# Turning the first sequence's rows in 32 x 32 squares on VectorE and moving them by DMA, in place of 16 TensorE transposes

## The chip, the cores and the metric

The kernel runs on one core of one Trainium2 chip. A core has TensorE (in the profile PE, with its weight loads as PEld), VectorE (DVE), ScalarE (ACT), GpSimd (POOL) and the sync engine (SP), which here only starts DMAs. ACT and POOL can start DMAs too. The metric is the device time of one launch in microseconds (us); less is better.

## The reference, cut to what matters

Two transformer layers run over an input x of 2 sequences x 512 rows x 512 columns, with a layer norm behind each of four parts: memory attention, a ternary feed-forward, softmax attention, a plain feed-forward. Only the end of the first part and the beginning of the second matter here:

```python
q_sel = (elu(x @ Wq.T + bq) + 1)[every 4th head]      # 8 heads of 128
num = einsum('bshd,hde->bshe', q_sel, M)
den = einsum('bshd,hd->bsh', q_sel, z) + 1e-6
x = layernorm(x + repeat(num / den, 4 heads) @ Wo.T)   # "reading"
gate, up = (x / 128) @ w_gate.T, (x / 128) @ w_up.T    # first feed-forward
x = layernorm(x + trunc(clip(down(trunc(silu(gate) * up)))))
```

The feed-forward truncates, so its products must be exact enough: each row x is split into a rounded part `hi` and a remainder `lo = x - hi`, and both are multiplied by the weights, which the kernel has found to be ternary.

## The kernel before, in words

**Tiles.** A sequence b is 4 tiles of 128 rows (`xs[b][t]`, 128 partitions x 512 columns, float32). The 8 tiles stand in the list `order`; tile i below is `order[i]`, so tiles 0 to 3 are the first sequence and 4 to 7 the second.

**The reading stage** is the loop `for i, (b, t) in enumerate(order)` at line 553. `read` (L419) makes, for tile i, 8 matmuls of 128 x 512 (L428), one for each head, into a PSUM bank each; there are 8 banks in all (`psum`, L81). They go in two groups of four heads, called g0 and g1 below. For each group ACT writes the four denominators (`den`, L432), DVE inverts them (L436), and then the banks are read: heads 0 to 2 by ACT into `y` (L441; three buffers), which POOL adds up (L445), and heads 3 to 7 by DVE, each with one instruction that adds into x (L450). Only then is a bank free for a head of the next tile. At the end POOL adds y into x (L457). The layer norm of tile i-1 lies within tile i (`norm_a0`, L526): statistics on DVE (L137, L139), the inverse root on POOL (L145, L146), an offset on DVE (`off`, L534), and the scaling of the row on ACT (L535).

**Turning the rows.** The feed-forward needs x with its columns on the partitions. For the first sequence TensorE did this: `split(0)` is called in tile 5, and its `block(k)`, two in tile 5 and two in tile 6, transposes four 128 x 128 blocks into a PSUM bank (L273), then ACT writes `hi` (L278) and DVE writes `lo` (L279) from that bank. For the second sequence DVE turns each tile in 32 x 32 squares as soon as it is normed (`turn_squares`, L549, instruction L551, into the tile `squares`), and `move_squares` (L284) then puts the squares in their places with 16 DMAs of 64 KB, in pieces of 128 bytes: 9 from SP's queue, 4 from POOL's, 3 from ACT's (L292). `split(1, xt1)` reads the result from SBUF behind the first four chunks of the feed-forward (L721).

**What sets the order.** POOL's instructions, and the DMAs that it starts, run as the program writes them (`manual_schedule`, L61). The instructions of PE, ACT and DVE are put in order by the framework's planner when the kernel is compiled; on the chip each engine then works through its list strictly in turn, and an instruction that must wait holds up all behind it. `tc.issue_after(x)` makes instructions of x's own engine stand behind x in that list.

**Buffers.** The pool `xtp` has two rooms of 128 x 2048 floats (tag `xt`), which are used in turn: the turned inputs `xt_a00` and `xt_a01`, then `xh_0` (the four `hi` blocks of the first sequence), then `squares`. The read queries are 16 tiles of 128 x 512 (tag `q`, L391), one for each sequence and head.

**Behind the reading stage**, `up(0, c)` for chunks c = 0 to 5 and then `up(1, 0)` multiply `hi` and `lo` by the weights (L611): per chunk four products of `hi` and four of `lo`, for the gate and again for the up part.

Of the kernel before, what the change touches and what calls it, by code (L numbers as in the profile page):

```python
# [10 lines left out]
F32 = mybir.dt.float32  # L11
# [8 lines left out]
P = 128  # L20
B, S, HID = 2, 512, 512
NT = S // P
NK = HID // P
NH, G, D = 8, 4, 128
# [6 lines left out]
SQ = 32  # L31
# [7 lines left out]
def kernel(  # L39
# [19 lines left out]
    nc = tc.nc  # L59
# [6 lines left out]
    xtp = ctx.enter_context(tc.tile_pool(name="xtp", bufs=2))  # L66
# [5 lines left out]
    ident = const.tile([P, P], F32, tag="ident", name="ident")  # L72
# [8 lines left out]
    def psum(name):  # L81
        return ps.tile([P, 512], F32, tag="mm", name=name)


    xs = [[], []]
# [171 lines left out]
            wds.append(wd)  # L257
        return wds

    def split(b, xt=None):  # L260


        hi = xtp.tile([P, NK, S], F32, tag="xt", name=f"xh_{b}").bitcast(F32R)
        los = [pair_tile(f"xl_{b}_{i}").bitcast(F32R) for i in range(2)]
        his = [hi[:, k, :] for k in range(NK)]
        los = [los[k // 2][:, k % 2, :] for k in range(NK)]

        def block(k):
            h, l = his[k], los[k]
            if xt is None:  # L270
                rows = psum(f"pt_f0{b}_{k}")
                for t in range(NT):
                    nc.tensor.transpose(rows[:, ts(t, P)], xs[b][t][:, ts(k, P)], ident)  # L273
            else:
                rows = xt[:, :, k, :]
                h, l = (u.rearrange("p (t q) -> p t q", t=NT) for u in (h, l))
            return (
                nc.scalar.copy(h, rows),  # L278
                nc.vector.tensor_sub(l, rows, h.bitcast(F32)),  # L279
            )  # L280

        return his + los, block
# [17 lines left out]
    def pair_tile(name):  # L300
        return wop.tile([P, 2, HID], F32, tag="wo", name=name)
# [6 lines left out]
    with tc.tile_pool(name="a0w", bufs=1) as a0w, tc.tile_pool(name="a0", bufs=2) as a0:  # L308
# [59 lines left out]
        def first_queries(pq, xt):  # L368

            done = first_rows(xt, 0)  # L370
            for t in range(NT):
                if t + 1 < NT:
                    with tc.issue_after(done.ins):
                        done = first_rows(xt, t + 1)
                with tc.issue_after(done.ins):
                    done = query_products(pq, xt, 0, ts(t, P))
            return done

        def queries(b, xt, h):

            pq = psum(f"pq_{b}_{h}")
            if b == h == 0:
                done = first_queries(pq, xt)
            else:
                done = query_products(pq, xt, h, slice(0, S))

            e = a0.tile([D, S], F32, tag="e", name=f"e_{b}_{h}")
            nc.scalar.activation(e, pq, AF.Exp, bias=bq[:, h : h + 1])  # L388
            r = a0.tile([D, S], F32, tag="r", name=f"r_{b}_{h}")
            nc.scalar.activation(r, pq, AF.Relu, bias=bq[:, h : h + 1])  # L390
            q = a0.tile([D, S], F32, tag="q", name=f"q_{b}_{h}", bufs=16)  # L391
            nc.vector.scalar_tensor_tensor(q, e, 1.0, r, ALU.min, ALU.add)
            qs[b].append(q)
            return done
# [84 lines left out]
            )  # L479

        checks = [(c, a) for c in range(len(CHUNKS)) for a in range(2)]
        qs = [[], []]
        xt = xtp.tile([P, NK, S], F32, tag="xt", name="xt_a00")
        with tc.issue_after(queries(0, xt, 0).ins):
            queries(0, xt, 1)
        for h in range(2, NH):
# [5 lines left out]
            elif h == 6:  # L492
                xt1 = transposed(xs[1], "a01")
# [31 lines left out]
        order = [(b, t) for b in range(B) for t in range(NT)]  # L525
# [23 lines left out]
        def turn_squares(i):  # L549
            b, t = order[i]  # L550
            nc.vector.transpose(squares[:, t, :], xs[b][t])  # L551

        for i, (b, t) in enumerate(order):
            steps = read(b, t, lambda steps: norm_a0(i - 1, steps) if i else None)
            for _ in range((3, 2, 2, 0, 0, 0, 0, 0)[i]):
                check_up(*checks.pop(0))
            if i == 3:
                tot_up = total(counts, "up")
            elif i == 4:
                flag_up, eff_up = verdict(tot_up, sc_up, "up")  # L560
            if i >= len(order) - LEAD:
                for a in range(2):
                    divided(i - len(order) + LEAD, a)
            if i == 5:
                parts, block = split(0)
                x2.append(parts)
                squares = xtp.tile([P, NT, HID], F32, tag="xt", name="squares")
            if i in (5, 6):
                for k in range(2):
                    block(2 * (i - 5) + k)  # L570
            if i > NT:
                turn_squares(i - 1)
        norm_a0(len(order) - 1, steps)
        turn_squares(len(order) - 1)
# [14 lines left out]
    xt1 = fp.tile([P, NT, NK, P], F32, tag="it11", name="xt_f01", bufs=1)  # L589
# [4 lines left out]
    with tc.tile_pool(name="f0", bufs=2) as f0:  # L594
# [123 lines left out]

        for c in range(LEAD - 2):
            up(0, c, [cut_off[f"f00_{c - 2}"]] if c > 1 else ())  # L720
        parts, block = split(1, xt1)  # L721
# [157 lines left out]
    for b in range(B):  # L879
# [5 lines left out]
        xt = xt_a1[b]  # L885
# [4 lines left out]
        for j in range(2):  # L890
            p = psum(f"pqk_{b}_{j}")
# [11 lines left out]
        for t in range(NT):  # L903
            p = psum(f"pv_{b}_{t}")
# [167 lines left out]
    t = NT - 1  # L1072
# [161 lines left out]
    steps = [(0, 0), (0, 1), (0, 2), (1, 0), (1, 1), (1, 2)]  # L1234
# [86 lines left out]
```

## Time and profile before

| What | us |
|---|---|
| median of 3 runs (lowest, highest) | 470.58 (470.02, 470.64) |
| the profiled execution's own time | 470.72 |
| its span in the trace | 468.7 |
| PE busy in the span | 461.0 (98%) |
| reading matmuls L428, 128 records | 57.1 |
| PE transposes of the first sequence L273, 16 records | 114.7 to 123.8 from the span's start |
| first product of the feed-forward | from 131.2 |
| DMAs of the second sequence's squares, started | 141.2 to 148.2 |
| first product of the second sequence | from 153.0 |

The profiled execution took 2.0 us more than its span, which is what lies around it. The granted clock of TensorE was 0.998. In the lists of the trace each line has a start in us from the span's start, a length in us, the engine, the line of the kernel and what it writes from what it reads; in square brackets stands how long the engine had been idle before and who ended that. A float32 matmul of the reading is recorded as two, so 8 heads are 16 records.

### The profile page before, as it was taken

How to read it: one execution, taken by the hardware profiler on the slowest of the kernel's cores; microseconds unless marked ns; L12 is line 12 of the kernel's file. 1: busy time of each engine (PE TensorE's matmuls, PEld its weight loads, DVE VectorE, ACT ScalarE, POOL GpSimd, SP SyncE). 2: the span in 40 equal slices, each digit the busy share in tenths (PEclk: the TensorE clock that was granted, in tenths of full speed). 3: DMA queues.
4: the chain of work that ended last, by engine and by line, in shares of the span. 5: the costliest groups of instructions: out<-in, count | busy, mean ns of one | idle time of the engine just before them, and what ended most of it. 6: DMA issues, size and time to landing. Idle time of an engine off the chain costs nothing.

```text
span 468.7 us, 5727 instructions
## 1 busy us (share of the span) xinstructions
PE 461.0 (98%) x1883; PEld 329.0 (70%) x1883; DVE 329.5 (70%) x627; ACT 267.5 (57%) x507; POOL 115.1 (25%) x144
## 2 busy tenths in 40 slices
PE   9999999999999999999999999999999999999994
PEld 8454444434478888888866567888888888888884
DVE  1165677767876767775979889895755778998632
ACT  3344799557756767456756842584645768443101
POOL 0235101566543053600357032000000000050111
PEclk9999999999999999999999999999999999999999
DMA  8989900000006500051390000000000000001001
GB/s 284 381 297 363 387 9 0 0 0 3 1 1 134 201 1 3 11 162 45 91 390 31 0 1 1 1 0 1 1 0 1 0 1 1 1 24 45 37 31 45
DMA packets 21651, 35.02 MB, mean 75 GB/s; under 512 B 9840, under 2 KB 10736, under 8 KB 21616
## 3 DMA queue, kind: packets, MB, share of 16 engines
q1 hardware_dynamic: 19616, 33.73, 20.7%
q10 hardware_dynamic: 1872, 0.56, 0.5%
q8 instruction: 22, 0.36, 0.3%
q0 software_dynamic: 128, 0.26, 0.3%
q14 instruction: 13, 0.11, 0.1%
HBM read 31.40 MB, written 2.10 MB: 71 GB/s over the span
## 4 chain that ended last, share of the span: by engine, by line
PE 71%; ACT 7%; DVE 5%; issue 3%; POOL 0%; POOLq 0%; DVEq 0%; ACTq 0%
PE pm L1111 17%; PE pg_f L611 9%; PE pu_f L611 9%; PE pc L1111 8%; PE pdm L1199 7%; PE pd_f L666 4%; PE pdc L1199 4%; DVE x L450 3%; PE pqk L893 3%; PE po L428 2%; ACT y L441 2%; ACT t L463 2%; PE pv L906 2%; PE pot L989 1%; PE po L1005 1%
## 5 line engine op out<-in xcount | busy, mean ns | idle before, releaser
L428 PE MATMUL po<-mw,q 128*128 128x512 f32 x128 | 57.1, 598 | 0.3 <-DVE mv_a L139 0.2
L352 PE MATMUL pq<-xt_a,wq 128*128 128x512 f32 (+1 forms) x152 | 56.9, 526 | 0.0
L145 POOL TENSOR_TENSOR rstd_f<-mv_f,ln_eps 128x1 f32<-128x1 f32 x15 | 4.4, 293 | 169.3 <-DVE mv_f L1214 130.2
L428 PEld LDWEIGHTS po<-mw,q 128*128 128x128 f32 x128 | 22.9, 189 | 32.1 <-issue 17.7
L352 PEld LDWEIGHTS pq<-xt_a,wq 128*128 128x128 f32 x152 | 26.2, 190 | 27.4 <-issue 25.7
L1111 PE MATMUL pm<-r,ugu 128*128 128x512 f32 x152 | 37.7, 389 | 0.0
L1111 PE MATMUL pm<-r,it_early 128*128 128x512 f32 x144 | 36.7, 392 | 0.0
L1111 PEld LDWEIGHTS pm<-r,ugu 128*128 128x128 f32 x152 | 28.5, 188 | 5.9
L1111 PEld LDWEIGHTS pm<-r,it_early 128*128 128x128 f32 x144 | 27.0, 188 | 6.1 <-issue 0.5
L169 ACT ACTIVATE ta_f<-y_f,below_half 128x512 int8<-128x512 f32 (+1 forms) x22 | 15.9, 721 | 27.0 <-DVE y_f L157 26.7
L450 DVE SCALAR_TENSOR_TENSOR x<-po,den,x 128x511 f32<-128x511 f32 x40 | 29.8, 745 | 1.9
L1121 DVE SCALAR_TENSOR_TENSOR ev_q<-pm,ev_q 128x512 f32<-128x512 f32 x27 | 18.6, 688 | 14.4 <-PE pm L1111 14.4
L637 DVE SCALAR_TENSOR_TENSOR it_f<-tb_f,ta_f 128x512 fp32r<-128x512 int16 (+1 forms) x22 | 15.4, 702 | 18.3 <-ACT tb_f L170 18.3
L445 POOL TENSOR_TENSOR y<-y,y 128x511 f32<-128x511 f32 x16 | 20.3, 1271 | 31.5 <-ACT y L441 30.8
L388 ACT ACTIVATE e<-pq,bq 128x512 f32<-128x512 f32 x16 | 11.1, 692 | 24.1 <-PE pq L352 20.6
L611 PE MATMUL pg_f<-xh,tu 128*128 128x512 f32 x88 | 24.3, 398 | 0.0
L1120 ACT ACTIVATE ev_q<-pc 128x512 f32<-128x512 f32 x27 | 16.0, 593 | 14.2 <-PE pc L1111 14.1
L465 POOL TENSOR_SCALAR td<-wd,inv_down 128x512 fp32r<-128x512 f32 x11 | 18.2, 1668 | 22.1 <-DVE inv_down L205 22.1
L611 PE MATMUL pg_f<-xl,tu 128*128 128x512 f32 x88 | 23.6, 390 | 0.0
L611 PE MATMUL pu_f<-xh,tu 128*128 128x512 f32 x88 | 23.5, 389 | 0.0
L611 PE MATMUL pu_f<-xl,tu 128*128 128x512 f32 x88 | 23.5, 389 | 0.0
L1001 ACT ACTIVATE x<-x,off_f,rstd_f 128x512 f32<-128x512 f32 x7 | 5.7, 816 | 27.7 <-POOL off_f L1000 27.7
(315 smaller groups left out, 1087.5 us busy)
## 6 DMA issues: line engine op xcount, KB each, us to landing
gu<-in_gu SPq DMA_DIRECT2D x20, 512.0 KB, 7.9
wo<-in_wo SPq DMA_DIRECT2D x16, 512.0 KB, 6.9
wd<-in_wd SPq DMA_DIRECT2D x20, 256.0 KB, 4.5
wq<-in_wq SPq DMA_DIRECT2D x8, 256.0 KB, 4.9
x<-in_x SPq DMA_DIRECT2D x7, 256.0 KB, 5.4
out<-x SPq DMA_DIRECT2D x7, 256.0 KB, 2.0
wqkv<-in_wqkv SPq DMA_DIRECT2D x1, 768.0 KB, 10.8
xt_f<-squares SPq DMA_DIRECT2D x9, 64.0 KB, 2.4
```

The costliest lines, as they stand in the source:

```text
L169: nc.scalar.activation(a[:n], y, AF.Relu, bias=below_half[:n])
L352: done = nc.tensor.matmul(pq[:, at], wq[h][:, k, :], xt[:, k, at], start=(k == 0), stop=(k == NK - 1),)
L428: nc.tensor.matmul(po, qs[b][h0 + j][:, ts(t, P)], mw[:, h0 + j, :], start=True, stop=True,)
L445: nc.gpsimd.tensor_add(ys[0][:, :LAST], ys[0][:, :LAST], y[:, :LAST])
L450: steps.append(nc.vector.scalar_tensor_tensor(x[:, :LAST], four[j][:, :LAST], d, x[:, :LAST], ALU.mult, ALU.add))
L465: eng.tensor_scalar(out, w, factor, None, ALU.mult)
L611: nc.tensor.matmul(pp[a], t[:, a, i % NK, :], x2[b][i], start=(i == 0), stop=(i == 2 * NK - 1),)
L666: nc.tensor.matmul(pd, inter[b][c][:, ts(t, P)], td[c].bitcast(F32R), start=(c == 0), stop=(c == last),)
L1111: nc.tensor.matmul(p, w, x, start=(left[id(p)] == begun[id(p)]), stop=(left[id(p)] == 1))
L1120: nc.scalar.activation(ev, pc, AF.Copy, scale=CROSS)
L1121: nc.vector.scalar_tensor_tensor(ev, pm, MAIN, ev, ALU.mult, ALU.add)
L1199: nc.tensor.matmul(p[:, :w], got[j // 4][1][kind][:, j % 4], down_parts[j][kind][:, cols], start=(j == 0 and kind == kinds[0]), stop=(j == ...
```

## The change

The first sequence's rows are now turned as the second's are. After each of the tiles 1 to 4 (i), `turn_first(i - 1)` has DVE turn the tile that was normed last, in squares, into a new tile `squares0` of the pool `xtp`, laid out so that four row tiles' pieces of one square lie next to each other. At i = 4 `move_first` starts 16 DMAs of 64 KB in pieces of 512 bytes, 6 from POOL's queue and 10 from SP's, into `xt_f00`. This takes the room of the read queries of heads 0 to 3 of the first sequence, which are now one tile of four heads. The PE transposes are gone. The `hi` and `lo` instructions read `xt_f00` from SBUF, all four blocks are written in tile 7, and those of DVE stand behind the first L450 of tile 7. `squares` now takes the room of `squares0`, and `xh_0` that of `xt_a01`.

```diff
-    def split(b, xt=None):
+    def split(b, xt):
...
         def block(k):
-            h, l = his[k], los[k]
-            if xt is None:
-                rows = psum(f"pt_f0{b}_{k}")
-                for t in range(NT):
-                    nc.tensor.transpose(rows[:, ts(t, P)], xs[b][t][:, ts(k, P)], ident)
-            else:
-                rows = xt[:, :, k, :]
-                h, l = (u.rearrange("p (t q) -> p t q", t=NT) for u in (h, l))
+            rows, order = xt(k)
+            h, l = (
+                u.rearrange(f"p (t i c) -> p {order}", t=NT, c=SQ) for u in (his[k], los[k])
+            )
...
-            q = a0.tile([D, S], F32, tag="q", name=f"q_{b}_{h}", bufs=16)
+            if b == 1:
+                q = a0.tile([D, S], F32, tag="q", name=f"q_{b}_{h}", bufs=8)
+            else:
+                if h % 4 == 0:
+                    qs0.append(a0.tile([D, 4, S], F32, tag=f"q0_{h // 4}", name=f"q0_{h}", bufs=1))
+                q = qs0[-1][:, h % 4, :]
...
+        squares0 = xtp.tile([P, NK, P // SQ, NT, SQ], F32, tag="xt", name="squares0")
+
+        def turn_first(t):
+            out = squares0.rearrange("p k j t c -> p (k j) t c")[:, :, t, :]
+            nc.vector.transpose(out, xs[0][t].rearrange("p (b c) -> p b c", c=SQ))
+
+        def move_first():
+
+            xt = a0.tile([P, NK, P // SQ, NT, SQ], F32, tag="q0_0", name="xt_f00", bufs=1)
+            for i in range(P // SQ):
+                for j in range(P // SQ):
+                    eng = nc.gpsimd if (4 * i + j) % 3 == 0 else nc.sync
+                    eng.dma_start(
+                        xt[ts(j, SQ), :, i].rearrange("p k t c -> p k (t c)"),
+                        squares0[ts(i, SQ), :, j].rearrange("p k t c -> p k (t c)"),
+                    )
+            return xt
...
             if i == 5:
-                parts, block = split(0)
+                parts, block = split(0, lambda k: (xt0[:, k], "i t c"))
                 x2.append(parts)
                 squares = xtp.tile([P, NT, HID], F32, tag="xt", name="squares")
-            if i in (5, 6):
-                for k in range(2):
-                    block(2 * (i - 5) + k)
-            if i > NT:
+            if i == len(order) - 1:
+                with tc.issue_after(steps[0].ins):
+                    for k in range(NK):
+                        block(k)
+            if 0 < i <= NT:
+                turn_first(i - 1)
+            if i == NT:
+                xt0 = move_first()
+            elif i > NT:
                 turn_squares(i - 1)
```

More of the change, by code (lines that the diff above doesn't have):

```diff
@@ L481 @@
         checks = [(c, a) for c in range(len(CHUNKS)) for a in range(2)]
-        qs = [[], []]
+        qs, qs0 = [[], []], []
         xt = xtp.tile([P, NK, S], F32, tag="xt", name="xt_a00")
@@ L720 @@
             up(0, c, [cut_off[f"f00_{c - 2}"]] if c > 1 else ())
-        parts, block = split(1, xt1)
+        parts, block = split(
+            1, lambda k: (xt1[:, :, k].rearrange("p t (i c) -> p t i c", c=SQ), "t i c")
+        )
         x2.append(parts)
```

## The prediction

> **What bounds the kernel now.** I read the page first: the busy times, then the shares of the chain that ended last.
>
> ```profile
> PE 461.0 (98%) x1883; PEld 329.0 (70%) x1883; DVE 329.5 (70%) x627; ACT 267.5 (57%) x507; POOL 115.1 (25%) x144
> ...
> PE 71%; ACT 7%; DVE 5%; issue 3%; POOL 0%; POOLq 0%; DVEq 0%; ACTq 0%
> ```
>
> TensorE is the bound almost everywhere. A share of the whole says nothing of this stage, so next the chain of waits around the edit (start, us, what):
>
> ```profile
> 116.50 0.75 DVE x L450
> 117.25 0.06 DVE st_a L137
> 117.31 0.46 issue
> 117.77 0.73 DVE x L450
> ...
> 118.65 4.53 PE po L428 x10
> 123.18 0.88 PE pt_f L273 x8
> 124.05 1.73 PE po L428 x4
> ...
> 126.07 0.62 ACT tu L463
> 126.69 4.53 PE po L428 x10
> 131.22 1.86 PE pg_f L611 x8
> ```
>
> From 118.65 on the chain lies on PE, the removed transposes (L273) are a link of it, and it runs on into the feed-forward (L611) without a hole. So PE time taken out before 131.2 moves the end, if nothing else becomes late. Then the timeline of 112 to 131, for what is near to being late:
>
> ```profile
> 113.19 0.81 ACT L535 ACTIVATE x<-x,off,rstd_a 128x512 f32<-128x512 f32 x1 [0.59 <-DVE off L534]
> 115.23 2.62 POOL L445 TENSOR_TENSOR y<-y,y 128x511 f32<-128x511 f32 x2 [0.84 <-ACT y L441]
> 116.22 0.18 DVE L436 RECIPROCAL den<-den 128x4 f32<-128x4 f32 x1 [2.12 <-ACT den L432]
> 118.67 0.19 POOL L145 TENSOR_TENSOR rstd_a<-mv_a,ln_eps 128x1 f32<-128x1 f32 x1 [0.82 <-DVE mv_a L139]
> 121.00 0.20 DVE L534 TENSOR_SCALAR off<-mv_a,rstd_a 128x1 f32<-128x1 f32 x1
> ```
>
> DVE has a hole of 2.12 us before the second reciprocal of tile 5, and POOL little room between its adds and the root that DVE's `off` needs. Last, the existing turn and move, as the tile `squares` shows them (ns min/median/max, first and last start):
>
> ```profile
> L292 SPq DMA_DIRECT2D xt_f<-squares x9: 627/645/1769, 141.3 to 148.2; - x9
> L551 DVE STREAM_TRANSPOSE squares<-x x4: 694/711/712, 122.1 to 140.4; 128x512 f32<-128x512 f32 x4
> L292 POOL DMA_DIRECT2D xt_f<-squares x4: 648/654/996, 141.9 to 144.2; - x4
> ```
>
> **The change part by part.** The sum is made against the profiled execution, 470.72 (span 468.7 and 2.0 around it); the median shown, 470.58, is 0.14 lower.
>
> *Transposes removed.* In the timeline eight of them occupy PE from 114.72 to 115.59, the next eight from 123.02 to 123.89: 0.87 each, **-1.75** in all, on the chain.
>
> *What they drag behind them.* A reading record costs 0.43 on PE (weight loads at 113.00, 113.43, 113.86), 16 of them 6.88. From 115.59 to 123.02 stand 16 records: 7.43, so 0.55 is lost; from 123.89 to the last one's end slot (about 131.05) 7.16, 0.28 lost. PE waits there for banks, held because casts (L278, 0.55 apart) and subtractions (L279, 0.66) stand between the denominators and the L450s, and because two banks hold transposed rows. In tile 6 casts and subtractions are gone afterwards: **-0.55**. In tile 7 four of each come instead of two: I count the 0.28 as kept.
>
> *DVE: four turns, 0.71 each if the spread-out writing costs nothing.* That pattern is not in the trace; the nearest rows of 512 columns are 0.68 (L137) and 0.75 (L450), so 2.7 to 3.0 for four. After the scaling of its tile (ACT L535) ends at 93.0, 100.3 and 114.0, DVE stands idle until 95.38, 102.55 and 116.22: three of four are covered. Tile 2's scaling ends at 107.83, amid the verdict; there the second reciprocal of tile 4 (109.26) slips by about 0.5, but PE has its banks of tile 5 in hand (no wait shown from 107.8 to 114.7). Cost 0; without that cover 0.7.
>
> *16 DMAs.* They can start when tile 3 is turned: 114.0 + 0.1 + 0.71 = 114.9. SP has nothing else to start before 141. A DMA with 128 pieces is not shown from SBUF to SBUF; a load with 128 rows starts every 0.49 (8 in 3.94 at 148.9), those with 512 pieces every 0.83 (9 in 7.50). I take 0.49, since the number of pieces is equal: ten are started by 119.8. Landing took 2.1 to 4.4, so the rows are there at 121.9 to 124.2, at worst (0.83, 4.4) 127.6. The casts want them at about 124 to 127.
>
> *POOL.* Its six DMAs go in front of tile 5's adds. By its row, 0.65 and 0.08 between: 4.4 us; by the load row of SP, 0.33 and 0.08, 2.5. They run from 114.9 (POOL is idle from 114.4 to 115.23), so the adds end at 120.0 to 121.9 in place of 117.85, and the root of tile 4, with 0.9, is ready at 120.9 to 122.8. `off` and behind it L535 of tile 4 want it at 119.8 (121.00 less two subtractions that leave). Against 1.1 to 3.0 us of lateness stands slack: without transposes PE reaches tile 7's first head at 122.4, when that bank would have been free since 121.55, so 0.85 is free. If the planner puts the reciprocal and the y's of tile 6 ahead of this `off`, as it put L436 and an L450 ahead of `off` at 105.6, the lateness costs nothing. So 0 to 2.1; I take **0**, as the planner sees POOL's list, and keep 2.1 for the range.
>
> [...]
>
> *Room of `squares`.* It is now that of `squares0`, so the turn of tile 4 (122.08 before, about 121 now) must wait until the DMAs have read it. DVE's hole there lasts to about 122.7: 0 if landed by 122, 1.5 at 124.2 if this turn stands first; I take 0.
>
> *The end of the stage.* PE is through with tile 7 at 131.05 - 2.3 = 128.75 and wants the first `lo` 0.91 later (four products of `hi`), the fourth at 130.34. DVE's first L450 of tile 7 (129.42 before) ends at about 127.8; four subtractions, 0.61 apart (2.50 for four from SBUF at 151.58), end at 130.25. If the turn of tile 5 stands ahead of them, 130.96: **+0.6**. I take that; it is 0 without. The casts (4 x 0.55) must then fit into ACT's list ahead.
>
> *Second sequence.* DVE's subtractions and turn (3.16) stand where a turn and 1.47 of idling stood (2.18), so its last turn comes 2.3 - 0.98 = 1.3 earlier, PE 1.7 earlier. Its last `lo` ended at 154.08 and was wanted at 153.02 + 0.91 + 0.68 = 154.61: the 0.53 of slack covers the 0.4. Cost 0.
>
> Sum: -1.75 - 0.55 + 0.6 = -1.7; 470.72 - 1.7 = **469.0**.
>
> [...]
>
> **The rivals.**
>
> *(a) POOL gives it back.* `off` of tile 4 stays ahead of tile 6's reciprocal, and DVE waits for the root behind six DMA issues. For it: program order on POOL, and the gap of only 0.8 before 115.23. Against it: the planner has swapped such pairs. Price up to 2.1: 469.0 + 2.1 = 471.1 at worst, with mid prices 470.5. PE's waits would then name y or L450 in tile 7.
>
> *(b) Slower: ACT's casts reach the head of its list before the rows land.* Only DVE's half is tied behind tile 7's first L450; ACT's is free to stand among the denominators of tile 6, at about 119.3. ACT is then held to the landing, 121.9 to 124.2, and with it the y's that free the banks; less 0.85 of slack, 1.8 to 4.1: about 472 (-1.7 + 3). It decides if the casts stand before tile 6's y's and the landing is after 121.5. Against it: the planner counts DMA time as well.
>
> *(c) The loop of DVE and ACT takes over from PE.* Tile 2 to 3 took 7.17 between second reciprocals (95.38 to 102.55), tiles 6 and 7 8.04. If they fall to 7.17 and no further, the gain is 1.74 in place of 2.3: 469.6 with the 0.6 at the end. Against it: tiles 4 and 5 ran at 6.7 and 7.0.
>
> *(d) It doesn't do what it says.* Hardly possible: the instructions are gone from PE's list.
>
> **How the numbers follow.** The forecast (468.2 to 469.5) 0.45; (c) 0.13; (a) 0.22; (b) 0.15; the rest, 0.05, a gain beyond 2.3. A change of under 0.2%, 0.94 us, can hardly be told from none. Faster: 0.45 + 0.13 and a part of the rest, 0.60; the same: (a), 0.22; slower: (b) and the worst of (a), 0.18. The range reaches from all of 1.75 + 0.83 and no wait (468.1) to (a) at its worst (471.2), and leaves out (b).
>
> **What would show it.** Right: no L273; the feed-forward's first product at about 129.5 in place of 131.2, all of the gain before it and the same distance from there to the end. (a): a long wait of DVE's `off` for the root around 120, POOL's issues right before. (b): ACT's cast with an idle time ended by a DMA. Room: L551 of tile 4 waiting for a DMA. End: PE's weight load of `pg_f` waiting for `xl`. The prediction is wrong above all if the six issues on POOL or the landing lie on the chain.

## The result and the profile after

The changed kernel takes 477.89 us (median of 5 runs, 476.30 to 477.99), the kernel before 470.58 beside it: a ratio of 1.0142, 95% interval 1.0131 to 1.0154. It is 1.4% slower. The forecast was 469.0, in a range up to 471.2, so it has the wrong sign, and the time lies beyond every rival. The profiled execution took 476.74, its span is 475.0. Below, L numbers are those of the changed kernel: L429 is the reading matmul (L428 before), L437 the reciprocal, L442 y, L446 and L458 POOL's adds, L451 DVE's adds, L274 and L275 the `hi` casts and `lo` subtractions, L535 `off`, L567 the new DMAs, L636 the products of the feed-forward. In the experiments they shift by a few lines. A gate product is eight matmuls, four of `hi` and four of `lo`; an up product is the same for the up part.

From the page of the changed kernel, the busy times and the chain's shares:

```profile
PE 462.6 (97%) x1867; PEld 328.2 (69%) x1867; DVE 333.9 (70%) x631; ACT 267.7 (56%) x507; POOL 119.5 (25%) x150
...
PE 74%; DMA 8%; ACT 5%; DVE 5%; issue 3%; POOL 2%; SPq 2%; POOLq 0%; DVEq 0%; ACTq 0%
```

PE has 16 instructions fewer (1867 for 1883) and is busy 1.6 us longer. DVE's busy time grew by 4.4, though four turns at 0.71 make only 2.8. So instructions have become longer on both engines. The chain's shares now name POOL and SP's queue with 2% each, but no place; that is found in the timeline of PE, from the last heads of the reading on:

```profile
125.31 1.13 PE L429 MATMUL po<-mw,q 128*128 128x512 f32 x2 [0.56 <-ACT y L442]
...
130.84 0.96 PE L636 MATMUL pg_f<-xh,tu 128*128 128x512 f32 x3
132.98 0.51 PE L636 MATMUL pg_f<-xh,tu 128*128 128x512 f32 x1 [1.18 <-ACT xh L274]
133.32 0.62 PE L636 MATMUL pg_f<-xl,tu 128*128 128x512 f32 x2
135.06 0.80 PE L636 MATMUL pg_f<-xl,tu 128*128 128x512 f32 x1 [1.12 <-DVE xl L275]
137.63 0.80 PE L636 MATMUL pg_f<-xl,tu 128*128 128x512 f32 x1 [1.78 <-DVE xl L275]
```

What follows, from the chain that ended last, before the change and then after it:

```profile
133.07 1.82 PE pu_f L611 x8
134.89 1.81 PE pg_f L611 x8
```

```profile
138.43 3.36 PE pu_f L636 x8
141.79 1.82 PE pg_f L636 x8
```

Two things are to be seen. The reading ends at 130.84, only 0.4 earlier than before (131.22), where 2.3 had been forecast. Then the first gate product, 1.86 before, takes from 130.84 to 138.43, because PE waits for the fourth cast and for two subtractions; and the eight matmuls of the up product behind it take 3.36 in place of 1.82 although they wait for nothing. The second gate product starts at 141.79 (134.89 before): 6.9 us late, of which 6.3 is left at the end of the span (475.0 against 468.7). DVE's list shows why the subtractions are late:

```profile
123.34 0.21 DVE L535 TENSOR_SCALAR off<-mv_a,rstd_a 128x1 f32<-128x1 f32 x1 [2.14 <-POOL rstd_a L146]
...
130.43 1.21 DVE L275 TENSOR_TENSOR xl<-xt_f,xh 128x512 fp32r<-128x512 f32 x1
131.56 0.70 DVE L552 STREAM_TRANSPOSE squares<-x 128x512 f32<-128x512 f32 x1
132.19 1.13 DVE L275 TENSOR_TENSOR xl<-xt_f,xh 128x512 fp32r<-128x512 f32 x1
133.24 0.17 DVE L437 RECIPROCAL den<-den 128x4 f32<-128x4 f32 x1
133.33 1.67 DVE L275 TENSOR_TENSOR xl<-xt_f,xh 128x512 fp32r<-128x512 f32 x1
134.93 0.74 DVE L451 SCALAR_TENSOR_TENSOR x<-po,den,x 128x511 f32<-128x511 f32 x1
...
136.93 0.65 DVE L275 TENSOR_TENSOR xl<-xt_f,xh 128x512 fp32r<-128x512 f32 x1
```

The four subtractions are strung out over tile 7's second group, and three of them take 1.13 to 1.67 where the fourth, alike in form, takes 0.65. POOL's list beside it:

```profile
116.36 3.51 POOL L567 DMA_DIRECT2D xt_f<-squares  x6 [1.46 <-PE po L429]
119.89 2.62 POOL L446 TENSOR_TENSOR y<-y,y 128x511 f32<-128x511 f32 x2
...
129.81 1.27 POOL L458 TENSOR_TENSOR x<-x,y 128x511 f32<-128x511 f32 x1 [0.80 <-DVE x L451]
131.04 1.73 POOL L446 TENSOR_TENSOR y<-y,y 128x511 f32<-128x511 f32 x1
```

The six issues stand ahead of tile 5's adds and make `off` of tile 4 wait 2.14: rival (a), in part. And the long subtractions at 130.43 to 135.0 lie beside POOL's adds of 129.81 to 134.4 (one L458, then two of L446, which take 1.67 each on the mean in place of 1.27).

So four suspects, each with an opposite: **order** (the subtractions and casts stand too late in DVE's and ACT's lists), **contention** (DVE's subtraction from SBUF beside POOL's adds), **POOL's issues** (rival a), and **the clock** (up products slowed behind the waits).

### The profile page after: what moved, and what is told of

It is laid out like the page before. It is cut to its first block, busy times and chain, and to the rows that moved or that the text cites. A ratio compares the mean times of both kernels' runs of the same rounds, so it can differ in the third digit from the quotient of the medians.

```text
span 475.0 us, 5758 instructions
## 1 busy us (share of the span) xinstructions
PE 462.6 (97%) x1867; PEld 328.2 (69%) x1867; DVE 333.9 (70%) x631; ACT 267.7 (56%) x507; POOL 119.5 (25%) x150
## 4 chain that ended last, share of the span: by engine, by line
PE 74%; DMA 8%; ACT 5%; DVE 5%; issue 3%; POOL 2%; SPq 2%; POOLq 0%; DVEq 0%; ACTq 0%
PE pm L1138 17%; PE pu_f L636 9%; PE pg_f L636 8%; PE pc L1138 8%; PE pdm L1226 7%; PE po L429 6%; PE pd_f L691 4%; PE pdc L1226 4%; DMA wo<-in_wo 3%; PE pqk L920 3%; DMA wqkv<-in_wqkv 2%; DVE x L451 2%; ACT t L464 2%; DMA gu<-in_gu 2%; PE pv L933 2%
## 5 line engine op out<-in xcount | busy, mean ns | idle before, releaser
L429 PE MATMUL po<-mw,q 128*128 128x512 f32 x128 | 57.1, 599 | 1.4 <-ACT y L442 0.6
L429 PEld LDWEIGHTS po<-mw,q 128*128 128x128 f32 x128 | 23.0, 189 | 34.7 <-issue 18.2
L451 DVE SCALAR_TENSOR_TENSOR x<-po,den,x 128x511 f32<-128x511 f32 x40 | 29.8, 745 | 1.7
L446 POOL TENSOR_TENSOR y<-y,y 128x511 f32<-128x511 f32 x16 | 21.1, 1316 | 29.0 <-ACT y L442 28.2
L636 PE MATMUL pg_f<-xl,tu 128*128 128x512 f32 x88 | 24.7, 399 | 2.9 <-DVE xl L275 2.9
L636 PE MATMUL pg_f<-xh,tu 128*128 128x512 f32 x88 | 24.3, 396 | 1.2 <-ACT xh L274 1.2
L636 PE MATMUL pu_f<-xh,tu 128*128 128x512 f32 x88 | 24.4, 400 | 0.0
L636 PE MATMUL pu_f<-xl,tu 128*128 128x512 f32 x88 | 24.3, 399 | 0.0
L636 PEld LDWEIGHTS pg_f<-xl,tu 128*128 128x128 f32 x88 | 16.7, 190 | 7.2 <-DVE xl L275 3.8
```

The costliest lines, as they stand in the source:

```text
L429: nc.tensor.matmul(po, qs[b][h0 + j][:, ts(t, P)], mw[:, h0 + j, :], start=True, stop=True,)
L446: nc.gpsimd.tensor_add(ys[0][:, :LAST], ys[0][:, :LAST], y[:, :LAST])
L451: steps.append(nc.vector.scalar_tensor_tensor(x[:, :LAST], four[j][:, :LAST], d, x[:, :LAST], ALU.mult, ALU.add))
L636: nc.tensor.matmul(pp[a], t[:, a, i % NK, :], x2[b][i], start=(i == 0), stop=(i == 2 * NK - 1),)
```

## The experiments

"Second gate product" below is its start, set against 134.89 of before, after the traces were laid upon each other at reciprocals that lie ahead of the change's effects (they differ by up to 0.7, and the result is good to about 0.1). It says what the end of the reading cost; the time says what was left of it at the end.

| Kernel | time, us | ratio to before (95%) | second gate product |
|---|---|---|---|
| the change | 477.89 | 1.0142 (1.0131 to 1.0154) | +6.9 |
| e1 POOL's DMAs on ACT | 479.28 | 1.0179 (1.0162 to 1.0196) | +8.8 |
| e10 all DMAs on SP | 478.86 | 1.0184 (1.0167 to 1.0201) | +6.9 |
| e2 without tile 7's POOL adds | 476.10 | 1.0093 (1.0058 to 1.0127) | +5.4 |
| e4 waits filled | 476.61 | 1.0123 (1.0106 to 1.0140) | +5.1 |
| e9 blocks ahead of tile 7 | 474.83 | 1.0091 (1.0074 to 1.0108) | +5.5 |
| e3 subtractions first | 473.47 | 1.0061 (1.0045 to 1.0078) | +4.0 |
| e8 blocks early, all on SP | 473.34 | 1.0059 (1.0043 to 1.0076) | +2.1 |
| e7 = e3 without those adds | 470.42 | 0.9998 (0.9988 to 1.0007) | +0.65 |
| e5 before, with turns and DMAs | 471.29 | 1.0019 (1.0009 to 1.0028) | +1.4 |
| e12 before, without those adds | 470.37 | 1.0000 (0.9991 to 1.0010) | 0.0 |
| e11 no turns, no DMAs | 469.10 | 0.9970 (0.9961 to 0.9980) | -1.4 |
| e13 three late issues on POOL | 472.02 | 1.0023 (1.0009 to 1.0037) | +1.8 |
| e16 = e13, wait filled | 470.92 | 1.0002 (0.9993 to 1.0011) | +0.35 |
| e14 = e13, adds behind | 475.34 | 1.0099 (1.0083 to 1.0114) | -0.8 |
| e15 = e14, turn behind too | 475.17 | 1.0096 (1.0081 to 1.0112) | -1.4 |
| e17 = e14, no address moved | 469.86 | 0.9980 (0.9971 to 0.9989) | -0.8 |
| e18 = e17, turn behind too | 469.76 | 0.9976 (0.9967 to 0.9985) | -1.4 |

### POOL's issues: e1, e10, e5

The first test put POOL's six DMAs on ACT's queue.

```diff
-                    eng = nc.gpsimd if (4 * i + j) % 3 == 0 else nc.sync
+                    eng = nc.scalar if (4 * i + j) % 3 == 0 else nc.sync
```

> The changed kernel with POOL's six DMAs started from ACT's queue, SP's ten left. Theory P (POOL's six issues, 3.5 us at 116.4 to 119.9, hold the root of tile 4 and tile 5's y adds, and PE pays about 2 us of it in tile 7): the first product of the feed-forward moves from 130.8 to about 129, DVE's wait of 2.1 us for that root is gone, and the time falls by 1.5 to 2.5 us. Rival E (only the end of the stage counts: lo blocks late because of DVE's order and of slow subtractions): the stage before becomes quicker but the last lo comes as late as before, and the time falls by less than 0.7.

479.28: slower still. It was no clean undoing, since the planner put the six issues among tile 5's denominators. ACT's timeline:

```profile
115.96 4.00 ACTq L567 DMA_DIRECT2D xt_f<-squares  x6
120.01 1.02 ACT L433 ACTIVATE den<-po,den_eps 128x1 f32<-128x1 f32 x6 [3.81 <-DMA xt_f<-squares]
```

An issue costs 0.67 of the issuing engine there, 0.585 on POOL. Six of them held the denominators behind them for 3.81, and these feed the banks at once: PE waited 2.6 for L451, and the reading ended 2.5 later than in the change. e10 moves them to SP, which has nothing else to do.

```diff
-                    eng = nc.gpsimd if (4 * i + j) % 3 == 0 else nc.sync
+                    eng = nc.sync
```

> The change with one word altered: all sixteen DMAs on SP's queue, none on POOL's. POOL is then free for tile 5's adds and tile 4's root. Theory P (POOL's six issues ate what the removed transposes gained before the end of the reading): reading ends at 128.6 to 129 in place of 130.84, with PE's 32 records of tiles 5 to 7 in one run. Rival (DVE and ACT's own loop holds the reading): 130.5 to 131. In both the rows land later (128.5 in place of 124.3), and the casts and subtractions stay where the change has them or later, so the first gate product should again wait 3 to 5 us: time 476 to 478.5 by theory P with the end of the stage unmended, since the end is set by DVE's list and not by PE.

PE's timeline of e10:

```profile
110.56 18.62 PE L429 MATMUL po<-mw,q 128*128 128x512 f32 x43
131.43 1.83 PE L636 MATMUL pg_f<-xh,tu 128*128 128x512 f32 x3 [2.25 <-ACT xh L274]
```

43 records without a hole, at 0.43 each: the reading ends at 129.2, in the change's own count 129.0, so theory P holds and **POOL's six issues had cost 1.8 of the 2.3 forecast**. The time did not follow (478.86, 0.4 above the range): PE now came earlier to the same late casts. And no subtraction of e10 stood beside an add of POOL (0.66 to 0.68 each), yet the last ended at 137.7: the lists alone make it late. e5 asks for the price of turns and DMAs where nothing at the end is late: the kernel before, with both added and their result unused.

```diff
+            if 0 < i <= NT:
+                turn_first(i - 1)
+            if i == NT:
+                xt0 = move_first()
-            if i > NT:
+            elif i > NT:
                 turn_squares(i - 1)
```

> The kernel before with the four turns of the first sequence and the sixteen DMAs added, whose result nobody reads: the first sequence's rows still come by TensorE's transposes, so DVE's and ACT's lists keep the order of before. Theory P (POOL's six issues, 3.5 us ahead of tile 5's adds, make the root of tile 4 and its `off` late, whatever the rest does): 2 us less the slack of 0.9 that the prediction gave, so 471.7 to 472.5, with an idle time of DVE's `off` of tile 4 ended by POOL. Theory N (the block hides, what was lost came from the end of the stage alone): 470.6, within 0.5. The clock after the stage should stay at 1.00 in both, since nothing waits for late subtractions.

471.29, 0.8 more than before: just above theory N's range and below theory P's. The wait that theory P named is there, in DVE's timeline of e5, and most of it is absorbed:

```profile
122.43 0.21 DVE L539 TENSOR_SCALAR off<-mv_a,rstd_a 128x1 f32<-128x1 f32 x1 [1.36 <-POOL rstd_a L146]
```

### Order and contention: e3, e2, e7, e12, e9

e3 has the blocks written between the two groups of tile 7; that puts all subtractions ahead of the second reciprocal and all casts ahead of tile 7's y's.

```diff
             for h0 in range(0, NH, 4):
+                if h0 and (b, t) == order[-1]:
+                    with tc.issue_after(steps[0].ins):
+                        for k in range(NK):
+                            behind = split0[0](k)
                 four = []
...
-            if i == len(order) - 1:
-                with tc.issue_after(steps[0].ins):
-                    for k in range(NK):
-                        block(k)
```

> The changed kernel with the four hi and lo blocks written into the program between the two groups of tile 7, so that DVE's list has the four subtractions ahead of the second reciprocal and the second group's L450s, and ACT's list has all four casts ahead of tile 7's y's; POOL unchanged. Theory O (order): the wait for the fourth cast (1.2 us) and most of the wait for the last lo (1.8 of 2.9) go, and with short waits the slow matmuls behind them: the time falls by 3 to 5 us. Rival C (contention): POOL's adds now meet all four subtractions, which stay at 1.1 to 1.7, and the time falls by less than 2.5.

473.47: **order alone is worth 4.4**, a part of the clock's loss included (the up product takes 2.87 in place of 3.36). e2 keeps the change's lists and leaves out POOL's two adds of y's in tile 7 (heads 1 and 2 are missing from that tile's sum).

```diff
-                        if ys:
+                        if ys and (b, t) != order[-1]:
                             nc.gpsimd.tensor_add(
```

> The changed kernel without POOL's two y adds (L446) of tile 7, so heads 1 and 2 are missing from that tile's rows; the order of DVE's list around the lo subtractions is unchanged. Theory C (a subtraction with both inputs in SBUF and a POOL add that reads SBUF hold each other up: 1.21, 1.13 and 1.67 us beside POOL's adds, 0.65 without): the second and third subtraction take about 0.65, the last lo comes 1.5 to 2 us earlier, the time falls by 1.5 to 3. Rival O (it is the order alone: five other DVE instructions stand between the third and fourth subtraction): the durations stay above 1 us, or the time falls by less than 0.7.

The subtractions of e2, from DVE's timeline, without POOL beside them:

```profile
130.69 1.21 DVE L275 TENSOR_TENSOR xl<-xt_f,xh 128x512 fp32r<-128x512 f32 x1
...
132.45 0.65 DVE L275 TENSOR_TENSOR xl<-xt_f,xh 128x512 fp32r<-128x512 f32 x1
...
133.10 0.66 DVE L275 TENSOR_TENSOR xl<-xt_f,xh 128x512 fp32r<-128x512 f32 x1
```

1.13 and 1.67 have become 0.65 and 0.66; the first, beside tile 6's L458, which is still there, keeps its 1.21. That shows contention in size. The time gained 1.8 by the medians, which is rough: the four executions of e2 lie between 473.12 and 476.53. Both edits together are e7 (it leaves out the same two adds, though the expectations of e7 and e12 count four).

> The changed kernel with the blocks between the two groups of tile 7 (as in the run with the subtractions first, 473.5) and without POOL's adds of tile 7's y's (two heads in each group are missing from that tile's sum). Order and contention theories together: the four subtractions go from 0.90 and 3.85 for three to 0.65 each, the last ends about 1.5 to 2 earlier, time 471.5 to 472.2. If the second sequence's rows are the next bound, the gain is given back at its casts: 473.0 to 473.5, with weight loads of the second sequence's products waiting for xh or xl at 152 to 160.

470.42, below the range: of the whole loss nothing is left, and the second edit was worth 3.05 on top of the first, more than alone. About 1.0 of it is the clock's, which the range had not counted: the up product takes 2.87 in e3 and 1.86 in e7, at a mean clock of 0.67 and of 1.00 in 135 to 139. The rest is the subtractions. The same three subtractions, from DVE's timelines of e3 and of e7:

```profile
130.90 3.85 DVE L275 TENSOR_TENSOR xl<-xt_f,xh 128x512 fp32r<-128x512 f32 x3
```

```profile
131.29 1.85 DVE L275 TENSOR_TENSOR xl<-xt_f,xh 128x512 fp32r<-128x512 f32 x3
```

e12 is the control: the kernel before with the same adds left out.

> Control for the runs without POOL's adds: the kernel before with the same four adds of tile 7 left out. Contention theory: before subtracts from PSUM, ends its subtractions ahead of these adds and gains nothing: 470.3 to 470.7. Rival (the adds themselves cost time, so that the gain of leaving them out says nothing of the subtractions): 468.5 to 469.5.

470.37 against 470.36. The adds as such cost nothing; what e7 gained came from the subtractions.

That earlier isn't always better shows e9, with the blocks ahead of tile 7, so that the four subtractions precede both its reciprocals:

```diff
+            if i == len(order) - 1:
+                with tc.issue_after(steps[-1].ins):
+                    for k in range(NK):
+                        block(k)
             steps = read(b, t, lambda steps: norm_a0(i - 1, steps) if i else None)
```

> The changed kernel with the blocks written ahead of tile 7, DMAs on SP and POOL as in the change (landed at 124.3). All four casts and subtractions stand ahead of tile 7's reciprocals. Order theory: no wait for xl at the first gate product; up to 2.6 us (four subtractions) of delay in tile 7's reciprocals, part of it in DVE's holes; 471 to 472.5. Rival (the banks of tile 7 are now held by the delayed reciprocals, so the wait only changes its place): 473 to 474, with PE's heads of tile 7 waiting for L451 or y.

474.83, above both ranges. The rival is right that the wait only changes its place, but it is the gate product and not tile 7's heads that waits, and its price was set too low. PE waits, from the list of its waits:

```profile
PE pg_f L636 <- ACT y L442: 3.9, 1, 3.9
```

The subtractions are done, but the banks of tile 7's heads, which the gate product needs, come free 3.9 late, because the reciprocal stands behind the subtractions. e8 has the same edit and all DMAs on SP; their later landing lets the planner put an L451 and the first reciprocal ahead of the subtractions.

> The changed kernel with all sixteen DMAs on SP and the blocks written ahead of tile 7 (casts ahead of tile 7's denominators, subtractions behind tile 7's first L451 and ahead of its second reciprocal). POOL then has nothing in the way of tile 4's root. DMAs 0.68 apart from 115.7 are issued by 126.6 and landed by about 128.7. Theory (order, POOL and contention together explain the loss): reading ends 1 to 2 earlier than in the change if ACT isn't held, subtractions done by 131 to 132; 470 to 471.5, the best of these. Rival (the prediction's (b)): the casts stand at the head of ACT's list from about 124 and hold tile 7's denominators until 128.7: 473 to 475, with ACT's cast idle for some 3 us behind a DMA.

PE's timeline of e8:

```profile
107.78 20.86 PE L429 MATMUL po<-mw,q 128*128 128x512 f32 x48
130.32 2.06 PE L636 MATMUL pg_f<-xh,tu 128*128 128x512 f32 x4 [1.68 <-ACT xh L274]
```

48 records in 20.86, and the reading ends at 128.64, 2.6 earlier than before: the forecast's gain is there in full. It is given back at once: 1.68 to the casts, which ACT reached at 129.65, 2.3 to a gate product paced by casts (0.52 apart) and by the subtractions, of which the first took 1.57 beside POOL's adds and the others 0.68, 0.7 to the clock in the up product (mean clock 0.68 in 131 to 135 and 0.89 in 135 to 139). 473.34 lies in the rival's range, but not by its mechanism: ACT's casts show no idle time behind a DMA.

### The gain alone: e11

Turns and DMAs left out, the splitting put back into tiles 5 and 6; it takes the normed rows untransposed, so that the first sequence's feed-forward sees other numbers.

```diff
-                parts, block = split(0, lambda k: (xt0[:, k], "i t c"))
+                parts, block = split(0, lambda k: (xs[0][k], "(t i c)"))
...
+            if i in (5, 6):
+                for k in range(2):
+                    block(2 * (i - 5) + k)
```

> The gain alone: the changed kernel without the four turns and sixteen DMAs of the first sequence; the casts and subtractions take the normalised rows as they stand, untransposed (so the first sequence's feed-forward sees other numbers), and are written in tiles 5 and 6 as before the change. Forecast's own first two terms (1.75 of transposes and 0.55 of stall): 468.2 to 468.8, the reading ending near 128.7 and no wait at the first gate product. Rival (c) of the prediction (DVE and ACT's loop takes over): 469.4 to 469.8. If it comes out at 470.5, the removed transposes were worth nothing even with the rows on time.

469.10, a ratio of 0.9970, between the forecast's range and rival (c)'s: 1.3 gained, no wait anywhere at the end of the stage. That is less than the 1.75 + 0.55; the planner put three subtractions ahead of tile 5's first reciprocal in DVE's list, and its reading there was about 0.9 behind that of e8.

### The clock: e4

Needless products in the change's three waits (5, 5 and 7, into a bank that is overwritten), all else the same.

```diff
                     for i in range(2 * NK):
+                        if b == c == a == 0:
+                            for _ in range({3: 5, 6: 5, 7: 7}.get(i, 0)):
+                                nc.tensor.matmul(
+                                    pp[1], t[:, 0, 0, :], x2[b][0], start=True, stop=True
+                                )
```

> The changed kernel with 17 needless products put into the three waits of the first feed-forward product (5 ahead of the fourth hi, 5 ahead of the third lo, 7 ahead of the fourth lo; they write a bank that is written anew afterwards). DVE's and ACT's lists are unchanged. Theory K (the clock: PE's granted clock is 0.59 and 0.51 in 134 to 141.7, since PE stood idle, and the 8 products behind the last wait take 3.36 us in place of 1.82): the clock stays at 1.0, those 8 products take 1.8, the time falls by about 1.5. Rival: something else slows those products, and the time stays within 0.5 or rises by the filling.

Stretches of the change (first) and of e4. The columns are the stretch and its length, busy times of PE, PEld, DVE, ACT and POOL, then PE's granted clock, the DMA share and GB/s:

```profile
135.00:139.00 4.00, 2.16 (x4) 1.45 (x5) 3.90 (x8) 0.00 (x0) 1.09 (x2) 0.50 0.00 0
139.00:143.00 4.00, 4.00 (x14) 3.12 (x12) 3.04 (x8) 3.38 (x4) 0.74 (x2) 0.67 0.02 4
```

```profile
135.00:139.00 4.00, 3.52 (x15) 2.27 (x14) 3.90 (x8) 0.00 (x0) 1.10 (x2) 1.00 0.00 0
139.00:143.00 4.00, 4.00 (x19) 3.30 (x18) 2.95 (x7) 0.87 (x2) 0.74 (x2) 1.00 0.02 4
```

With PE kept busy the clock stays at 1.00 and the up product takes 1.86 again, so theory K holds for it: the second gate product is 1.75 earlier. Of the time 1.3 is gained by the medians; the two profiled executions are equal (476.75 and 476.74). What took it back shows in e4's waits: weight loads of the second sequence wait 1.7 in all for its casts and subtractions around 158, whose last squares were turned at 143.8 in that trace (143.25 in the change's, 140.45 before). So that chain is next in line, 2.8 late itself.

### A version that keeps the gain: e13, e16, e14, e15, e17, e18

e13 puts 13 DMAs on SP and three on POOL behind tile 5's last add, where POOL had a hole; the blocks are written as in e9.

```diff
+                    if (i == j < 3) == pool:
+                        eng = nc.gpsimd if pool else nc.sync
```

> A version that the runs so far point to: thirteen DMAs on SP and three on POOL behind tile 5's last add, where POOL had a hole of 0.84; casts and subtractions written ahead of tile 7, which puts them around tile 6's `off` on ACT and DVE and ahead of tile 7's second reciprocal. Rows landed at about 126. If order, POOL's block and the landing together explain the loss: reading ends at 128.6 to 129, subtractions done by 132, second gate product at 133.5 to 134.5, 469.5 to 470.3. If the subtractions beside POOL's adds decide (0.84 to 1.2 each in place of 0.65): 470.8 to 472. If the casts hold the y's of tile 7 as in the run with the blocks ahead of tile 7: 473 and more.

472.02, on two levels: three of nine executions at 470.3 to 470.8, the others at 471.9 to 472.5; the granted clock over the span is 0.996 to 0.998 in the three and 0.994 in the six. The reading ends at 128.6. Then PE's timeline:

```profile
133.32 0.60 PE L637 MATMUL pg_f<-xl,tu 128*128 128x512 f32 x1 [1.17 <-DVE xl L275]
133.72 1.91 PE L637 MATMUL pu_f<-xh,tu 128*128 128x512 f32 x4
135.42 1.81 PE L637 MATMUL pu_f<-xl,tu 128*128 128x512 f32 x4
```

One wait, and the eight matmuls of the up product take 3.31, at a granted clock of 0.75 to 0.82 in these stretches. e16 fills that wait with seven needless products.

> The run with three late issues, and seven needless products into the up product's bank ahead of the gate product's last two (two and five, 0.23 each), so that TensorE has work in the wait of 1.17; DVE's and ACT's lists unchanged. Clock theory: the granted clock stays at 1.00, the eight up products take 1.82 to 1.9 in place of 3.31, and all executions agree at 470.2 to 470.7. Rival (the two levels of 470.3 and 472.0 have another cause): two levels again, 472 in most.

470.92 (470.29 to 471.34), 0.2 over the range, with 1.86 for the eight, a clock of 1.00 and no upper level: the 1.1 between the medians is the clock's.

e14 mends the contention without leaving work out: POOL's two adds of tile 7 stand behind a POOL copy that reads the last subtraction's result.

```diff
+                held = small.tile([P, 1], F32, tag="held", name="held", bufs=1)
+                hold = nc.gpsimd.tensor_copy(held, parts[-1][:, :1].bitcast(F32))
...
+                                if (b, t) == order[-1]:
+                                    tied.enter_context(tc.issue_after(hold.ins))
```

> The run with three late issues (472.0, in some executions 470.3), and POOL's two adds of tile 7 held behind the last subtraction by one POOL instruction that reads it; nothing is left out. Contention theory: the three subtractions that took 2.92 together take about 2.0, the wait of 1.17 before the last product falls to 0.3 or less, and the clock stays: 469.6 to 470.4. The adds end at about 134.5, ahead of DVE's own add at 137. Rival (the stretching has another cause, such as the strided rows): 472.0 as before, with 0.97 for each subtraction still.

475.34. The stage did what was expected (no wait, the second gate product 0.8 earlier than before), yet the time is 3.3 over e13's. e15, with the turn of tile 5 behind the subtractions too, agrees: 475.17. e14 misses its range by 5.

> As e14, and the turn of tile 5 (0.70 on DVE, until now between the first and second subtraction) behind the fourth. If DVE's list still set the first gate product in e14, another 0.3 to 0.6 is gained: 469.2 to 470. If ACT's casts set it (one per 0.55 from about 128.5), the same as e14 within 0.3.

The chain of e14 behind the stage shows where it went:

```profile
133.54 1.85 PE pg_f L641 x8
135.40 1.86 PE pu_f L641 x8
```

Each eight products take 1.85 to 1.86 in place of 1.81 to 1.82, at a granted clock of 1.00, and so on to the kernel's end. The one thing that reaches so far is the new tile `held`: by the addresses in the compiled kernels the tiles behind it lie 32 bytes further than in e17 below, `tu` and `xl` at 32 beyond a multiple of 64 (the first `tu` at 132512 in place of 132480); `xh`, which lies ahead of it, stays where it was (89472, a multiple of 64). e17 and e18 put the value into a tile that was there already.

```diff
-                held = small.tile([P, 1], F32, tag="held", name="held", bufs=1)
+                held = small.tile([P, 1], F32, tag="col", name="held", bufs=2)
```

> As e14, with the held value in a small tile that the kernel had already, so all tiles lie where they lay in the run with three late issues. Address theory: eight products take 1.81 again, and with the waits gone the time is 475.3 less some 45 groups of products at 0.045 and what follows in the later stages: 469.2 to 470, under the time before. Rival (the extra POOL instruction or the order of the adds makes TensorE slower): 475 again, with 1.85 per eight products.

> As e15, with no address moved. Address theory: as the run beside it or up to 0.5 less, 469 to 470. Rival: 475 again.

469.86 and 469.76: **faster than before by 0.20% (0.11 to 0.29) and 0.24% (0.15 to 0.33)**, with the whole computation. The chain of e17:

```profile
132.22 1.86 PE pu_f L641 x8
134.08 1.82 PE pg_f L641 x8
135.91 1.81 PE pu_f L641 x8
```

And DVE's and POOL's timelines of e17 show the contention a last time:

```profile
128.07 1.20 DVE L275 TENSOR_TENSOR xl<-xt_f,xh 128x512 fp32r<-128x512 f32 x1
129.19 0.70 DVE L555 STREAM_TRANSPOSE squares<-x 128x512 f32<-128x512 f32 x1
129.81 1.85 DVE L275 TENSOR_TENSOR xl<-xt_f,xh 128x512 fp32r<-128x512 f32 x3
```

```profile
127.45 1.27 POOL L461 TENSOR_TENSOR x<-x,y 128x511 f32<-128x511 f32 x1 [0.65 <-DVE x L454]
131.73 0.19 POOL L580 COPY held<-xl 128x1 f32<-128x1 f32 x1 [3.01 <-DVE xl L275]
131.87 2.67 POOL L449 TENSOR_TENSOR y<-y,y 128x511 f32<-128x511 f32 x2
```

POOL's add ends at 128.72, the subtraction that began in it at 129.27, 0.55 later and 1.20 after its start; the three with POOL idle take 1.85, or 0.62 each. The adds now lie behind, in time for DVE's add at 135.98.

## Why the prediction was wrong, step by step

**"Transposes removed" and "what they drag" (-1.75, -0.55): right for the reading.** With POOL and the end of the stage mended, it ends at 128.6 (e8, e17), 2.6 earlier than before. At the end of the kernel no run shows more than 1.3 of it, with the rows on time and no move at all (e11), and 0.9 with the move (e18).

**"DVE: four turns, 0": right.** 0.71 each, in the holes named; up to about 118 nothing was lost.

**"16 DMAs": the landing right, the spacing not.** On SP ten took 6.77, 0.68 apart and not 0.49; the rows landed at about 124 (the last DMA started at 121.9, and these sixteen took 2.0 to 3.3 from start to landing), the late end of the forecast's 121.9 to 124.2. What the step missed is what landing at 124 means: the splitting, which had stood in the holes of tiles 5 and 6, could now only begin in tile 7, where DVE had none left.

**"POOL: I take 0": wrong; rival (a) named the right wait, though not its condition.** The planner did put a reciprocal and an L451 of tile 6 ahead of `off`, as was hoped, and it was not enough, for the y buffers and L536 hung on POOL too. Price: 1.8 of the reading (e10), 0.8 of the time where nothing else is late (e5), inside the bounds of 0 to 2.1.

**"The end of the stage: +0.6": the step that failed.** It came to 5.7 in the gate product and 1.5 behind it. Three parts. (1) It let the four subtractions follow the first L451 of tile 7 without a gap; in DVE's list a reciprocal, L451s and statistics stood between, the last subtraction ended at 137.6 and not at 130.25, and the fourth cast, which "must fit into ACT's list ahead", began at 132.28. Only one L451 was tied ahead; nothing tied the others behind. Worth 4.4 (e3). (2) Its 0.61 for a subtraction came from rows in which POOL was idle. Beside POOL's adds three took 1.13 to 1.67. Worth 1.8 in the change's order (e2), 3.05 once the order is mended (e3 to e7). (3) PE's waits were priced as waits; the clock's 1.5 behind them was not in the sum (e4). This 1.5 is not a third price beside the two: parts of it are contained in them.

What the traces show of (2): 0.65 without POOL, 1.20 beside an add that ended 0.65 into the subtraction (e17). Before the change the same subtraction read PSUM and took 0.66 in this stage, but there no such add ran beside it. In e5 one did (POOL's adds of 124.72 to 127.34, the subtraction at 126.18), and the subtraction from PSUM took 0.69. That both inputs lie in SBUF is what makes the difference is the author's reading of this one pair, 0.69 against 1.20; by what means POOL's adds lengthen the subtraction was not shown.

**"Second sequence: 0": wrong, but covered.** Its last turn came at 143.25, 2.8 later and not 1.3 earlier, as DVE's list had slipped. It cost nothing in the change, since PE was later still, and took part of what e4 won.

**"Room of `squares`": the 0 is right, but by luck.** The turn of tile 4 waited 0.88 for ACT's scaling, not for a DMA. It had no DMA to wait for: in e10 it ran at 121.39, while SP still had DMAs out of `squares0` to start (the same sixteen kept it from 114.82 to 126.09 in e8). It is `xh_0` that takes the room of `squares0`, and `squares` takes that of `xt_a01`; the text on the change has the two the wrong way round, and this term rests on it.

Rival (b) named the casts, but put the danger at the head of ACT's list; in the change they were late at its end. In e9 work put early held the banks, as (b) feared, but it was DVE's subtractions and not ACT's casts. One thing looks odd in the table: e2's profiled execution gained 1.4 at the second gate product and only 0.2 in time. Its half clock came later (about 135.5 to 142.3, in the change 134.8 to 141.6), so that the second gate product took 2.70 in place of 1.82; that is 0.9 of the 1.2. What stays open: the rest of it, and which operand slows the products of the later stages in e14.

## What to carry to other kernels

When a step is replaced by one that delivers its data later, price not only the new step but all that consumed the old data: find the holes that this work had stood in, and ask whether there are any left behind the landing. A duration is only good for the company it was measured in: a DVE instruction with both inputs in SBUF must be priced beside what POOL does in that stage (here 0.65 alone and up to 1.67 beside POOL's adds). A tie that puts one instruction ahead says nothing of the others; read from the planned list what will stand between. And a wait of TensorE can cost twice, once as a wait and once in the slower products behind it (in the change 1.5 in eight products, at a granted clock of 0.50).

## What the runs showed of the hardware

- **Contention.** A 128 x 512 subtraction with both inputs in SBUF: 0.65 alone, up to 1.67 beside POOL's 128 x 511 adds, which went from 1.27 to 1.67 each (the change). With one input in PSUM it took 0.69 beside such an add (e5).
- **Clock.** In the change PE waited 1.18 and then 1.12; from 134.8, within the second of these waits, the granted clock was 0.50 for 6.83 us, and eight products took 3.36 in place of 1.82. The clock of this trace is either 1.00 or 0.50 (values between are means over a stretch). From such means, over stretches of 4 us from 131 on, the half behind the reading works out at about 3.4 in e3, e8 and e13, 6.8 to 6.9 in e1, e2 and e9, and 10.2 in e10: about one, two and three times the same length. In the profiled execution of e13 a single wait of 1.17, with products 0.5 apart before it, was enough (mean clock 0.82 in 131 to 135, 0.75 in 135 to 139); six of nine executions have its clock over the span, 0.994, and three have 0.996 to 0.998. In e7, with no wait over 0.4 in this stage, and in e16 and e17, with none, the clock stayed at 1.00. What sets the length, and why it happens in some executions only, was not shown.
- **Addresses.** With tiles moved by 32 bytes eight products of 512 columns took 1.855 in place of 1.815 (2.2%), and products of the later stages slowed alike (L1143: 395 ns on the mean in place of 389): 5.5 us of the kernel's time (e14 against e17, 475.34 and 469.86, whose only difference is where the held value lies; e15 against e18, 475.17 and 469.76, show the same). The products of `xh`, which had not moved, slowed no less than those of `xl` (396 ns at the median in place of 389, against 393 in place of 389), so for them the moved operand is `tu`. The plain float32 products of the reading did not change (596 ns both).
- **Issuing.** A DMA of 128 pieces of 512 bytes from SBUF to SBUF cost its engine 0.585 to 0.63 on POOL (six in 3.51 in the change, three in 1.88 in e17; the record of one issue is 0.55 at the median and 0.79 at most in the change), 0.67 on ACT (six in 4.00 in e1), 0.68 to 0.70 on SP (ten in 6.77 in the change, sixteen in 11.27 in e8).
